# A time-mix layer and a GELU FFN in one kernel: the output projection of blocks two to seven set behind the FFN, around the next block's half chunk

## The chip, the cores and the metric

The kernel runs on one core of a Trainium2 chip. The metric is the device time of one execution in microseconds (us), the median of several runs. Engines are called as the profile calls them: PE is TensorE (matmul), PEld its weight loads, DVE is VectorE, ACT is ScalarE, POOL is GpSimd, and SP is the engine whose queue issues the DMAs.

## The reference

The input `x` is 4 x 1024 x 512, f32. It is normalised over its last axis, and two branches are computed from the result and added to `x`. The first is a time mix with a recurrence over the tokens, the second a GELU FFN with fp16 at three places.

```python
xn = layernorm(x)                                  # over 512
# branch 1, HIDDEN = 704
xx = concatenate([xn[:, 1:2], xn[:, :-1]], axis=1) - xn
k = (xn + xx * time_mix_k) @ Wk.T                  # 512 -> 704
r = (xn + xx * time_mix_r) @ Wr.T
w = exp(-exp(time_decay))
state = state * w + relu(k_t); out_t = state * r_t # a scan over the tokens
y = layernorm(out @ Wv.T) * gamma + beta           # 704 -> 512
# branch 2, N = 2048
X = xn.astype(float16)
D = gelu(X.astype(float32) @ W0.T + bias0).astype(float16)
E = (D.astype(float32) @ W1.T + bias1).astype(float16)
result = x + y + E
```

## The kernel before

The 4096 tokens are worked through in eight blocks of 512 (index `i` = 0 to 7 in the code; the text counts them from one). A block's work on PE is:

- `attention` (L361): the 704 hidden channels are five full chunks of 128 and a half chunk of 64. For each full chunk, `pk` and `pr` (L385) are products of four 128x128 pieces of the weights with 512 tokens, in f32, which the hardware runs as two matmuls each. ACT takes relu of `pk` into `rk` (L370), DVE scans it into `st` (L372), POOL copies the last state into `carry`, and DVE multiplies `st` and `pr` into `g` (L396). The half chunk puts k and r into the two halves of one bank, `both` (named `pkr`): its matmuls have 64 columns each (128*64 in the profile), one for k and one for r, on the two column halves of the array. Its result is `gh` (L408).
- `ffn` (L470): the sixteen up products `pd` (L480, f32r, eight matmuls each, weights in a high and a low part), GELU on ACT into `d16` (L488), a cast on DVE into `d` (L490), and sixteen down products onto the four banks `pe` (L495, eight matmuls each). Up runs two steps ahead of down.
- `attention_out` (L413): the projection of `g` and `gh` to 512 channels, one bank `po` for each of four stripes of 128 tokens. Full chunks are 128*128 matmuls (L420); the half chunk's have 64 rows (64*128, L430), two stripes side by side on the two row halves of the array. The order is: full chunks of stripes 0 and 1, all the half chunks, full chunks of stripes 2 and 3. `residual` then takes statistics (L183, L184), the reciprocal deviation on POOL (L177, L178) and three DVE operations (L441, L444, L445) into `z`; the first of them is the last reader of `po`.
- `finish` (L463): `pe` plus bias in fp16 (`e16`, L466), the sum with `z` (L467), and the DMA to `out`.

The dictionary `between` puts three steps into the loop over n of the FFN: at n = 0 the projection of the same block, at n = 4 the normalisation of the next block's `x` (`layernorm`, L183 to L187), at n = 7 its transposition into `xnT` (sixteen L204) and the mixed inputs `xk` and `xnT` (L348, L350). `finish` of block `i` comes behind its FFN, ahead of `attention` of block `i + 1`.

Engines run their instructions in the order given; a scheduler orders them at build time within what the tiles' dependencies allow, except in stretches of `manual_schedule`. PSUM has two pools of four banks: `ps_mm` for `pk`, `pr`, `pkr`, `pd` and `po`, and `ps_e` for `pe`. A tile takes the bank of the fourth tile before it in its pool, and its first matmul waits for that tile's last reader. `x`, `xk`, `g`, `gh` and `xnT` exist once; `xres` has two buffers, `z` four, `w1` three. The weights of down are read again from DRAM for each block (`w`, 512 KB for each n), on SP's queue, with `x`, `xres` and `out`.

Of the kernel before, what the change touches and what calls it, by code (L numbers as in the profile page):

```python
# [8 lines left out]
F16 = mybir.dt.float16  # L9
F32 = mybir.dt.float32  # L10
# [4 lines left out]
P = 128  # L15
# [4 lines left out]
def time_mix_and_gelu_ffn(  # L20
# [26 lines left out]
    nc = tc.nc  # L47
    B, T, C = x.shape
    HID = wkT.shape[1]
    N = w0T.shape[1]  # L50
    TB = 512
    NS = TB // P
    NC = C // P
# [4 lines left out]
    NF = HID // P  # L58
# [296 lines left out]
    def ffn_input(i, x16s):  # L355
        xf = wide.tile([P, NC, TB], F32R, tag="xf", name=f"xf_{i}")
        for c in range(NC):
            nc.vector.tensor_copy(xf[:, c, :], x16s[c])
        return xf

    def attention(i, xk):  # L361


        b, t0 = blocks[i]
        g = one.tile([P, NF, TB], F32, tag="g", name=f"g_{i}")
        gh = one.tile([P, NS // 2, P], F32, tag="gh", name=f"gh_{i}")

        def states(h, hw, pk):
            rk = two.tile([P, TB], F32, tag="rk", name=f"rk_{i}_{h}", bufs=1)
            nc.scalar.activation(rk[:hw], pk, AF.Relu)  # L370
            st = two.tile([P, TB], F32, tag="st", name=f"st_{i}_{h}")
            nc.vector.tensor_tensor_scan(  # L372
                st[:hw],
                w_sb[:hw, h : h + 1].to_broadcast([hw, TB]),
                rk[:hw],
                0.0 if t0 == 0 else carry[:hw, h : h + 1],
                ALU.mult,
                ALU.add,
            )
            if t0 + TB < T:  # L380
                nc.gpsimd.tensor_copy(carry[:hw, h : h + 1], st[:hw, TB - 1 : TB])
            return st

        def product(dst, w, cols, src, c):
            nc.tensor.matmul(dst, w[c][:, cols], src, start=(c == 0), stop=(c == NC - 1))  # L385

        for h in range(NF):
            cols = slice(h * P, (h + 1) * P)
            pk = ps_mm.tile([P, TB], F32, tag="mm", name=f"pk_{i}_{h}")
            for c in range(NC):  # L390
                product(pk, wk_sb, cols, xk[:, c, :], c)
            st = states(h, P, pk)
            pr = ps_mm.tile([P, TB], F32, tag="mm", name=f"pr_{i}_{h}")
            for c in range(NC):
                product(pr, wr_sb, cols, xnT[:, c, 1:], c)
            nc.vector.tensor_mul(g[:, h, :], st, pr)  # L396

        both = ps_mm.tile([P, TB], F32, tag="mm", name=f"pkr_{i}")
        for c in range(NC):
            product(both[:HF], wk_sb, slice(H0, HID), xk[:, c, :], c)  # L400
            product(both[HF:], wr_sb, slice(H0, HID), xnT[:, c, 1:], c)
        st = states(NF, HF, both[:HF])

        def tokens(ap, odd):
            return ap.rearrange("p (s two t) -> p s two t", two=2, t=P)[:, :, odd, :]

        for odd in range(2):
            nc.vector.tensor_mul(  # L408
                gh[odd * HF : (odd + 1) * HF], tokens(st[:HF], odd), tokens(both[HF:], odd)
            )  # L410
        return g, gh

    def attention_out(i, g, gh):  # L413

        b, t0 = blocks[i]
        pos = [ps_mm.tile([P, C], F32, tag="mm", name=f"po_{i}_{s}") for s in range(NS)]

        def full(s, first):
            for h in range(NF):
                nc.tensor.matmul(  # L420
                    pos[s],
                    g[:, h, s * P : (s + 1) * P],
                    wv_sb[:, h, :],
                    start=(first and h == 0),
                    stop=(not first and h == NF - 1),
                )

        def half(s, first):
            rows = slice(s % 2 * HF, (s % 2 + 1) * HF)
            nc.tensor.matmul(  # L430
                pos[s], gh[rows, s // 2, :], wv_sb[rows, NF, :], start=first, stop=not first
            )

        def residual(s):
            xr = two.tile([P, C], F32, tag="xres", name=f"xres_{i}_{s}")
            nc.sync.dma_start(xr, x[b, t0 + s * P : t0 + (s + 1) * P, :])
            mv = four.tile([P, 1, 2], F32, tag="mv1", name=f"mvy_{i}_{s}")
            stats_of(mv, 0, pos[s], f"sty_{i}_{s}")
            rstd = rstd_of(mv[:, :, 1], f"ry_{i}_{s}")
            z = four.tile([P, C], F32, tag="z", name=f"z_{i}_{s}")  # L440
            nc.vector.scalar_tensor_tensor(  # L441
                z, pos[s], mv[:, 0, 0:1], gamma_sb, ALU.subtract, ALU.mult
            )
            nc.vector.scalar_tensor_tensor(z, z, rstd, beta_sb, ALU.mult, ALU.add)  # L444
            nc.vector.tensor_add(z, z, xr)  # L445
            return z

        early, late = range(NS // 2), range(NS // 2, NS)  # L450
        for s in early:
            full(s, True)
        for s in early:
            half(s, False)
        for s in late:
            half(s, True)
        zs = [residual(s) for s in early]
        for s in late:
            full(s, False)
        zs += [residual(s) for s in late]  # L460
        return zs

    def finish(i, s, z, pe):  # L463
        b, t0 = blocks[i]
        e16 = two.tile([P, C], F16, tag="e16", name=f"e16_{i}_{s}")
        nc.vector.tensor_add(e16, pe, b1_sb)  # L466
        nc.vector.tensor_add(z, z, e16)  # L467
        nc.sync.dma_start(out[b, t0 + s * P : t0 + (s + 1) * P, :], z)

    def ffn(i, xf, between, state):  # L470


        pe = [ps_e.tile([P, C], F32, tag="pe", name=f"pe_{i}_{s}") for s in range(NS)]

        def up(n):
            pd = ps_mm.tile([P, TB], F32, tag="mm", name=f"pd_{i}_{n}")
            cols = slice(n * P, (n + 1) * P)
            for c in range(NC):
                for w in (w0h, w0l):
                    nc.tensor.matmul(  # L480
                        pd,
                        w[c][:, cols],
                        xf[:, c, :],
                        start=(c == 0 and w is w0h),
                        stop=(c == NC - 1 and w is w0l),
                    )
            d16 = two.tile([P, TB], F16, tag="d16", name=f"d16_{i}_{n}")
            nc.scalar.activation(d16, pd, AF.Gelu, bias=b0_sb[:, n : n + 1])  # L488
            d = wide.tile([P, TB], F32R, tag="d", name=f"d_{i}_{n}", bufs=4)
            nc.vector.tensor_copy(d, d16)  # L490
            return d

        def down(n, s, d, w1):
            for part in range(2):
                nc.tensor.matmul(  # L495
                    pe[s],
                    d[:, s * P : (s + 1) * P],
                    w1[part],
                    start=(n == 0 and part == 0),
                    stop=(n == NN - 1 and part == 1),  # L500
                )

        last = 3 if i == len(blocks) - 1 else 0
        AHEAD = 2
        waiting = [(up(n), load_w1(i, n)) for n in range(AHEAD)]
        for n in range(NN):
            if n in between:
                between[n]()  # L510
            if n + AHEAD < NN:
                waiting.append((up(n + AHEAD), load_w1(i, n + AHEAD)))
            if n < NN - last:
                operands = waiting.pop(0)
                for s in range(NS):
                    down(n, s, *operands)
        if last:
            with tc.manual_schedule(engines={nc.tensor.engine, nc.vector.engine}):
                for s in range(NS):
                    for n, operands in zip(range(NN - last, NN), waiting):  # L520
                        down(n, s, *operands)
                    finish(i, s, state["zs"][s], pe[s])
        return pe

    behind = ExitStack()
    x16s, xk = first_inputs(x_now, behind)
    xf = ffn_input(0, x16s)
    for i in range(len(blocks)):
        more = i + 1 < len(blocks)
        state = {}  # L530
        gs = attention(i, xk)
        if i == 0:
            for grp in range(N // W0G):
                load_w0(grp)
# [3 lines left out]
            x_now = load_x(i + 1)  # L538

        def out_stage():  # L540
            state["zs"] = attention_out(i, *gs)

        def next_norm():
            layernorm(i + 1, x_now)
# [2 lines left out]
            transposed(x_now)  # L547
            state["mixed"] = mixed_inputs(i + 1)

        between = {0: out_stage}  # L550
        if more:
            between[4] = next_norm
            between[7] = next_inputs
        pe = ffn(i, xf, between, state)
        if more:
            x16s, xk = state["mixed"]
            xf = ffn_input(i + 1, x16s)
            for s in range(NS):
                finish(i, s, state["zs"][s], pe[s])


# [41 lines left out]
```

## Time and profile before

| | us |
|---|---|
| median of 4 runs | 944.89 (944.73 to 945.22) |
| profiled execution, its own time | 944.73 |
| its span (granted PE clock 1.0 throughout) | 942.8 |
| busy: PE / PEld / DVE / ACT / POOL | 934.4 / 587.5 / 485.8 / 162.7 / 51.8 |
| `pd` (L480), two rows | 203.5 + 199.4, 1024 matmuls, mean 397 and 389 ns |
| `pe` (L495) | 251.1, 1024 matmuls, mean 389 ns |
| `pr`, `pk` (L385) | 144.2 and 144.1, 320 matmuls each, mean 592 ns |
| `po` full chunks (L420) / half chunk (L430) | 140.8, 320 matmuls / 15.9, 64 matmuls |
| `pkr` (L385), two rows | 29.2 + 29.2, 64 matmuls each, mean 598 and 599 ns |
| DMA | 106.49 MB, mean 113 GB/s |

The span is the stretch that the profile covers; the time of the execution is 1.9 us longer. Busy times of a group count overlapping matmuls of the group once, so the mean duration of a matmul (592 ns in f32) is longer than the step from one to the next; the step is read from start times. Blocks follow each other evenly: in the chain of waits `pk` of block three begins at 244.76 us, that of block four at 360.29, and so on every 115.52 us. One block's stretches, with the busy time and the instructions (x) of each engine in them:

```
core 0: us, PE busy (x) PEld busy (x) DVE busy (x) ACT busy (x) POOL busy (x), PEclk, DMA share, GB/s
244.76:279.04 34.28, 34.28 (x81) 14.81 (x79) 12.43 (x15) 2.98 (x5) 0.93 (x5) 1.00 0.18 56
279.04:282.63 3.59, 3.59 (x17) 1.07 (x16) 0.69 (x1) 0.00 (x0) 0.00 (x0) 1.00 0.02 5
282.63:286.41 3.78, 3.78 (x18) 3.11 (x17) 2.49 (x4) 1.28 (x2) 0.18 (x1) 1.00 0.01 2
286.41:305.70 19.29, 19.29 (x50) 8.20 (x49) 8.98 (x16) 0.69 (x1) 2.91 (x6) 1.00 0.11 27
305.70:360.10 54.40, 54.40 (x241) 45.06 (x240) 34.63 (x65) 11.60 (x18) 2.07 (x4) 1.00 0.50 166
```

They are: the five full chunks, the half chunk, two up products, the projection, and the rest of the FFN. PE is busy through all of them.

### The profile page before, as it was taken

Reading aid. Unit: us, or ns where it says so; the run is one execution under the profiler, and the core shown is the slowest. Engines: PE = TensorE matmul, PEld = TensorE weight load, DVE = VectorE, ACT = ScalarE, POOL = GpSimd, SP = SyncE. Lnnn points to the kernel's source line nnn. Section 1 sums busy time; section 2 is a strip of 40 time slices with the busy share of each in tenths; the row PEclk is TensorE's granted clock in tenths of the full one; section 3 lists DMA queues with packets and bytes.
Section 4 is the critical chain, followed back from the end, with each engine's and each line's share of the span. In section 5 each row is a group of like instructions: output and inputs, shape, how many; then the busy total and the mean of one; then the engine's idle time right before and its main releaser. Section 6 shows DMA issues by size and latency. Waiting matters only on the chain.

```text
span 942.8 us, 8746 instructions
## 1 busy us (share of the span) xinstructions
PE 934.4 (99%) x3260; PEld 587.5 (62%) x3260; DVE 485.8 (52%) x842; ACT 162.7 (17%) x265; POOL 51.8 (5%) x124
## 2 busy tenths in 40 slices
PE   8999999999999999999999999999999999999998
PEld 5447764488544885448854588445884458744686
DVE  6558752484425944359343592426923279332513
ACT  6323410012100220102201021010210102111021
POOL 0010000100001000011000100002000020000100
PEclk9999999999999999999999999999999999999999
DMA  9744660045401454014530155302552024510243
GB/s 296 231 138 151 226 232 0 23 134 188 147 1 24 138 197 133 1 33 159 188 111 1 38 182 167 105 0 68 185 159 81 0 89 135 161 62 1 69 154 112
DMA packets 39573, 106.49 MB, mean 113 GB/s; under 512 B 4431, under 2 KB 4460, under 8 KB 39532
## 3 DMA queue, kind: packets, MB, share of 16 engines
q1 hardware_dynamic: 39532, 105.94, 34.4%
q8 instruction: 26, 0.43, 0.2%
q14 instruction: 15, 0.12, 0.0%
HBM read 89.14 MB, written 16.78 MB: 112 GB/s over the span
## 4 chain that ended last, share of the span: by engine, by line
PE 94%; DVE 4%; issue 1%; DMA 0%; ACT 0%; POOL 0%; SPq 0%; DVEq 0%
PE pd L480 23%; PE pe L495 22%; PE po L420 15%; PE pr L385 15%; PE pk L385 15%; PE pkr L385 3%; PE po L430 2%; DVE xnT L204 1%; DVE w L125 0%; DMA x<-in_L_attn_x 0%; DVE d L490 0%; DVE z L467 0%; DVE xk L350 0%; DVE e L466 0%; DVE stx L183 0%
## 5 line engine op out<-in xcount | busy, mean ns | idle before, releaser
L495 PE MATMUL pe<-w,d 128*128 128x512 f32 x1024 | 251.1, 389 | 1.4 <-DVE w L125 0.8
L495 PEld LDWEIGHTS pe<-w,d 128*128 128x128 f32 x1024 | 192.1, 188 | 42.3 <-DVE d L490 1.5
L480 PE MATMUL pd<-xf,w0h 128*128 128x512 f32 x512 | 203.5, 397 | 0.0
L480 PE MATMUL pd<-xf,w0l 128*128 128x512 f32 x512 | 199.4, 389 | 0.0
L488 ACT ACTIVATE d<-pd,b_sb 128x512 f16<-128x512 f32 x128 | 87.9, 687 | 418.6 <-PE pd L480 408.4
L385 PE MATMUL pr<-xnT,wr 128*128 128x512 f32 x320 | 144.2, 592 | 0.0
L385 PE MATMUL pk<-xk,wk 128*128 128x512 f32 x320 | 144.1, 592 | 0.0
L420 PE MATMUL po<-wv_sb,g 128*128 128x512 f32 x320 | 140.8, 595 | 0.0
L490 DVE CAST d<-d 128x512 fp32r<-128x512 f16 x128 | 53.9, 423 | 130.2 <-ACT d L488 129.3
L480 PEld LDWEIGHTS pd<-xf,w0h 128*128 128x128 f32 x512 | 96.1, 188 | 28.0 <-issue 5.7
L480 PEld LDWEIGHTS pd<-xf,w0l 128*128 128x128 f32 x512 | 96.1, 188 | 21.4 <-issue 1.9
L385 PEld LDWEIGHTS pr<-xnT,wr 128*128 128x128 f32 x320 | 60.6, 189 | 76.9 <-issue 75.7
L420 PEld LDWEIGHTS po<-wv_sb,g 128*128 128x128 f32 x320 | 60.1, 190 | 75.7 <-issue 74.7
L385 PEld LDWEIGHTS pk<-xk,wk 128*128 128x128 f32 x320 | 60.7, 190 | 73.3 <-issue 72.0
L204 DVE STREAM_TRANSPOSE xnT<-x 32x512 f32<-32x512 f32 x112 | 78.7, 703 | 2.2
L372 DVE TENSOR_TENSOR_SCAN st<-w_sb,carry,rk 128x512 f32<-128x512 f32 (+1 forms) x24 | 30.8, 1282 | 70.3 <-ACT rk L370 70.3
L370 ACT ACTIVATE rk<-pk 128x512 f32<-128x512 f32 x40 | 23.9, 597 | 233.6 <-PE pk L385 233.6
L183 DVE BATCH_NORM_STATS2 sty<-po 128x6 f32<-128x512 f32 x32 | 22.0, 689 | 73.5 <-PE po L430 67.9
L372 DVE TENSOR_TENSOR_SCAN st<-w_sb,rk 128x512 f32<-128x512 f32 (+1 forms) x24 | 29.3, 1221 | 55.3 <-ACT rk L370 53.6
L396 DVE TENSOR_TENSOR g<-st,pr 128x512 f32<-128x512 f32 x40 | 27.4, 686 | 53.6 <-PE pr L385 53.6
L177 POOL TENSOR_SCALAR ry<-mvy 128x1 f32<-128x1 f32 x32 | 11.4, 357 | 502.3 <-DVE mvy L184 502.3
L466 DVE TENSOR_TENSOR e<-pe,b_sb 128x512 f16<-128x512 f32 x32 | 20.7, 684 | 17.0 <-PE pe L495 17.0
(75 smaller groups left out, 457.2 us busy)
## 6 DMA issues: line engine op xcount, KB each, us to landing
w<-w1d SPq DMA_DIRECT2D x111, 512.0 KB, 3.3
x<-in_L_attn_x SPq DMA_DIRECT2D x32, 256.0 KB, 3.0
xres<-in_L_attn_x SPq DMA_DIRECT2D x32, 256.0 KB, 2.6
w1d<-w SPq DMA_DIRECT2D x16, 512.0 KB, 2.9
out<-z SPq DMA_DIRECT2D x32, 256.0 KB, 5.5
w0raw<-in_L_ffn_W SPq DMA_DIRECT2D x16, 256.0 KB, 4.8
w1raw<-in_L_ffn_W SPq DMA_DIRECT2D x16, 256.0 KB, 3.6
wk<-in_L_attn_Wk SPq DMA_DIRECT2D x4, 352.0 KB, 4.4
```

What stands on the lines that cost most here:

```text
L183: nc.vector.bn_stats(st6, src)
L204: nc.vector.transpose(dst[i * Q : (i + 1) * Q, :, :, j, :], src[j * Q : (j + 1) * Q, :, :, i, :],)
L370: nc.scalar.activation(rk[:hw], pk, AF.Relu)
L372: nc.vector.tensor_tensor_scan(st[:hw], w_sb[:hw, h : h + 1].to_broadcast([hw, TB]), rk[:hw], 0.0 if t0 == 0 else carry[:hw, h : h + 1], A ...
L385: nc.tensor.matmul(dst, w[c][:, cols], src, start=(c == 0), stop=(c == NC - 1))
L396: nc.vector.tensor_mul(g[:, h, :], st, pr)
L420: nc.tensor.matmul(pos[s], g[:, h, s * P : (s + 1) * P], wv_sb[:, h, :], start=(first and h == 0), stop=(not first and h == NF - 1),)
L466: nc.vector.tensor_add(e16, pe, b1_sb)
L480: nc.tensor.matmul(pd, w[c][:, cols], xf[:, c, :], start=(c == 0 and w is w0h), stop=(c == NC - 1 and w is w0l),)
L488: nc.scalar.activation(d16, pd, AF.Gelu, bias=b0_sb[:, n : n + 1])
L490: nc.vector.tensor_copy(d, d16)
L495: nc.tensor.matmul(pe[s], d[:, s * P : (s + 1) * P], w1[part], start=(n == 0 and part == 0), stop=(n == NN - 1 and part == 1),)
```

## The change

`attention` is split into two functions, `full_chunks` and `half_chunk`, which it returns uncalled. The half chunk's bank `both` moves from `ps_mm` to `ps_e`. `attention_out` takes a function `amid` and calls it between the half chunk's matmuls and the late full chunks. `finish` is split: `rounded` makes `e16` (four buffers instead of two) and frees the bank of `pe`. For blocks two to seven `between` no longer holds the projection; behind the FFN come the four `rounded`, the next block's `xf`, the projection with the next block's half chunk in the middle, the four `finish`, and then the next block's full chunks. Block one and block eight keep their projection at n = 0 of the FFN; block two's half chunk stays behind its full chunks. The scheduler sets the steps of `between` (the next block's normalisation and transposition) anew where the engines' orders leave room: on DVE they come earlier than before, the statistics and the normalisation in the projection and the full chunks before, the transposes from the first casts of the FFN on.

```diff
@@ -361,9 +361,8 @@
     def attention(i, xk):
         b, t0 = blocks[i]
-        g = one.tile([P, NF, TB], F32, tag="g", name=f"g_{i}")
-        gh = one.tile([P, NS // 2, P], F32, tag="gh", name=f"gh_{i}")
         def states(h, hw, pk):
             rk = two.tile([P, TB], F32, tag="rk", name=f"rk_{i}_{h}", bufs=1)
@@ -384,33 +383,42 @@
         def product(dst, w, cols, src, c):
             nc.tensor.matmul(dst, w[c][:, cols], src, start=(c == 0), stop=(c == NC - 1))
-        for h in range(NF):
-            cols = slice(h * P, (h + 1) * P)
-            pk = ps_mm.tile([P, TB], F32, tag="mm", name=f"pk_{i}_{h}")
-            for c in range(NC):
-                product(pk, wk_sb, cols, xk[:, c, :], c)
-            st = states(h, P, pk)
-            pr = ps_mm.tile([P, TB], F32, tag="mm", name=f"pr_{i}_{h}")
-            for c in range(NC):
-                product(pr, wr_sb, cols, xnT[:, c, 1:], c)
-            nc.vector.tensor_mul(g[:, h, :], st, pr)
-        both = ps_mm.tile([P, TB], F32, tag="mm", name=f"pkr_{i}")
-        for c in range(NC):
-            product(both[:HF], wk_sb, slice(H0, HID), xk[:, c, :], c)
-            product(both[HF:], wr_sb, slice(H0, HID), xnT[:, c, 1:], c)
-        st = states(NF, HF, both[:HF])
+        def full_chunks():
+            g = one.tile([P, NF, TB], F32, tag="g", name=f"g_{i}")
+            for h in range(NF):
+                cols = slice(h * P, (h + 1) * P)
+                pk = ps_mm.tile([P, TB], F32, tag="mm", name=f"pk_{i}_{h}")
+                for c in range(NC):
+                    product(pk, wk_sb, cols, xk[:, c, :], c)
+                st = states(h, P, pk)
+                pr = ps_mm.tile([P, TB], F32, tag="mm", name=f"pr_{i}_{h}")
+                for c in range(NC):
+                    product(pr, wr_sb, cols, xnT[:, c, 1:], c)
+                nc.vector.tensor_mul(g[:, h, :], st, pr)
+            return g
         def tokens(ap, odd):
             return ap.rearrange("p (s two t) -> p s two t", two=2, t=P)[:, :, odd, :]
-        for odd in range(2):
-            nc.vector.tensor_mul(
-                gh[odd * HF : (odd + 1) * HF], tokens(st[:HF], odd), tokens(both[HF:], odd)
-            )
-        return g, gh
-    def attention_out(i, g, gh):
+        def half_chunk():
+            gh = one.tile([P, NS // 2, P], F32, tag="gh", name=f"gh_{i}")
+            both = ps_e.tile([P, TB], F32, tag="pe", name=f"pkr_{i}")
+            for c in range(NC):
+                product(both[:HF], wk_sb, slice(H0, HID), xk[:, c, :], c)
+                product(both[HF:], wr_sb, slice(H0, HID), xnT[:, c, 1:], c)
+            st = states(NF, HF, both[:HF])
+            for odd in range(2):
+                nc.vector.tensor_mul(
+                    gh[odd * HF : (odd + 1) * HF],
+                    tokens(st[:HF], odd),
+                    tokens(both[HF:], odd),
+                )
+            return gh
+        return full_chunks, half_chunk
+    def attention_out(i, g, gh, amid=lambda: None):
         b, t0 = blocks[i]
         pos = [ps_mm.tile([P, C], F32, tag="mm", name=f"po_{i}_{s}") for s in range(NS)]
@@ -454,16 +462,21 @@
             half(s, False)
         for s in late:
             half(s, True)
+        amid()
         zs = [residual(s) for s in early]
         for s in late:
             full(s, False)
         zs += [residual(s) for s in late]
         return zs
-    def finish(i, s, z, pe):
+    def rounded(i, s, pe):
+        e16 = four.tile([P, C], F16, tag="e16", name=f"e16_{i}_{s}")
+        nc.vector.tensor_add(e16, pe, b1_sb)
+        return e16
+    def finish(i, s, z, e16):
         b, t0 = blocks[i]
-        e16 = two.tile([P, C], F16, tag="e16", name=f"e16_{i}_{s}")
-        nc.vector.tensor_add(e16, pe, b1_sb)
         nc.vector.tensor_add(z, z, e16)
         nc.sync.dma_start(out[b, t0 + s * P : t0 + (s + 1) * P, :], z)
@@ -519,16 +532,21 @@
                 for s in range(NS):
                     for n, operands in zip(range(NN - last, NN), waiting):
                         down(n, s, *operands)
-                    finish(i, s, state["zs"][s], pe[s])
+                    finish(i, s, state["zs"][s], rounded(i, s, pe[s]))
         return pe
     behind = ExitStack()
     x16s, xk = first_inputs(x_now, behind)
     xf = ffn_input(0, x16s)
+    state = {}
+    full_chunks, half_chunk = attention(0, xk)
+    g = full_chunks()
+    gh = half_chunk()
     for i in range(len(blocks)):
         more = i + 1 < len(blocks)
-        state = {}
-        gs = attention(i, xk)
         if i == 0:
             for grp in range(N // W0G):
                 load_w0(grp)
@@ -538,7 +556,7 @@
             x_now = load_x(i + 1)
         def out_stage():
-            state["zs"] = attention_out(i, *gs)
+            state["zs"] = attention_out(i, g, gh)
         def next_norm():
             layernorm(i + 1, x_now)
@@ -547,16 +565,26 @@
             transposed(x_now)
             state["mixed"] = mixed_inputs(i + 1)
-        between = {0: out_stage}
+        within = i == 0 or not more
+        between = {0: out_stage} if within else {}
         if more:
             between[4] = next_norm
             between[7] = next_inputs
         pe = ffn(i, xf, between, state)
         if more:
             x16s, xk = state["mixed"]
+            e16s = [rounded(i, s, pe[s]) for s in range(NS)]
             xf = ffn_input(i + 1, x16s)
+            full_chunks, half_chunk = attention(i + 1, xk)
+            next_gh = []
+            if within:
+                zs = state["zs"]
+            else:
+                zs = attention_out(i, g, gh, lambda: next_gh.append(half_chunk()))
             for s in range(NS):
-                finish(i, s, state["zs"][s], pe[s])
+                finish(i, s, zs[s], e16s[s])
+            g = full_chunks()
+            gh = next_gh[0] if next_gh else half_chunk()
 # ---- launch: one core; the weights go in transposed ----
```

## The prediction

> **What bounds the kernel now.** I read the page first (busy shares, and the chain that ended last), then all waits of TensorE, then the chain again over one block, then TensorE's timeline where the tiling of the array changes. The page:
>
> ```profile
> span 942.8 us, 8746 instructions
> ...
> PE 934.4 (99%) x3260; PEld 587.5 (62%) x3260; DVE 485.8 (52%) x842; ACT 162.7 (17%) x265; POOL 51.8 (5%) x124
> ...
> PE 94%; DVE 4%; issue 1%; DMA 0%; ACT 0%; POOL 0%; SPq 0%; DVEq 0%
> ```
>
> TensorE is the bound nearly throughout. All that it waited for in the span:
>
> ```profile
> PE idle L231 <- POOL ident masks.py:199: 1.3, 1, 1.3
> PE pt L254 <- ACT x L248: 1.3, 1, 1.3
> PE pe L495 <- DVE w L125: 0.8, 1, 0.8
> PE pe L495 <- DVE d L490: 0.6, 2, 0.3
> ```
>
> (us in total, times, longest). Two lie in the prologue, two in block one's FFN and at the very end; in blocks two to seven TensorE never waits. A change there can gain only by making TensorE's own instructions take less, and can lose by creating a wait. The chain over block three's start (start, us, what) shows where its instructions take more than their step:
>
> ```profile
> 275.68 3.44 PE pr L385 x8
> 279.11 3.59 PE pkr L385 x16
> 282.70 3.87 PE pd L480 x16
> 286.58 8.59 PE po L420 x20
> 295.16 1.92 PE po L430 x8
> 297.08 8.78 PE po L420 x20
> ```
>
> An f32 product of 512 columns is two matmuls of 3.44/8 = 0.43 us. `pkr` holds 16 matmuls of half the columns which run in pairs: 8 x 0.43 = 3.44, but it took 3.59. The 16 `pd` would be 3.63 (the FFN's casts of `d` follow each other every 3.63 us, for 16 such matmuls), but took 3.87. The first 20 `po` fit (8.59); the half chunk's four pairs should be 1.72 and took 1.92; the last 20 took 8.78. The timeline shows the excess itself (start, us, instruction):
>
> ```profile
> 278.09 1.02 PE L385 MATMUL pr<-xnT,wr 128*128 128x512 f32 x2
> 279.04 0.64 PE L385 MATMUL pkr<-xk,wk 128*64 128x512 f32 x1
> ...
> 279.52 0.59 PE L385 MATMUL pkr<-xk,wk 128*64 128x512 f32 x1
> ...
> 282.10 0.59 PE L385 MATMUL pkr<-xk,wk 128*64 128x512 f32 x1
> ...
> 282.63 0.50 PE L480 MATMUL pd<-xf,w0h 128*128 128x512 f32 x1
> 282.97 0.39 PE L480 MATMUL pd<-xf,w0l 128*128 128x512 f32 x1
> 283.19 0.40 PE L480 MATMUL pd<-xf,w0h 128*128 128x512 f32 x1
> ```
>
> Into column pairs (128*64): after `pr` the next start is due at 278.09 + 2 x 0.43 = 278.95 and comes at 279.04 (+0.09); the second pair comes 0.48 after the first instead of 0.43 (+0.05): 0.14 us. Out of them: due at 282.53, comes at 282.63 (+0.10), and the second `pd` 0.34 later instead of 0.23 (+0.11): 0.21 us. Into the row pairs (64*128) 1.92 - 1.72 = 0.20, out of them 8.78 - 8.58 = 0.20. So each change of tiling costs about 0.1 us in which nothing overlaps, and then a first weight load that is not hidden: about 0.05 us where it has 64 columns, 0.1 us where it has 128. A block pays 0.14 + 0.21 + 0.20 + 0.20 = 0.75 us for four changes.
>
> **The change, part by part.** (1) *The merged excursion.* For blocks two to seven the projection (`po`) runs after the FFN, and the next block's `pkr` runs between its row pairs and the late full chunks. TensorE's order becomes: FFN, 20 `po`, row pairs, column pairs, 20 `po`, the ten full chunks. Count and kinds of matmuls are the same, and this order has three changes per merged pair where there were four: into rows (0.20), rows to columns, columns to full (its first load has 128 columns, so as out of the row pairs: 0.20). The trace of before has no change from rows straight to columns. From below it is 0 (no drain and a hidden load), from above the two dearest rows after each other, 0.20 + 0.20 = 0.40. I take 0.14, the row of another tiling into columns: the first load has the same 64 columns. New sum 0.54, saved 0.21 us, six times: **1.3 us**. With the bounds it is six times 0.35 = 2.1 us saved, or six times 0.05 = 0.3 us lost. Switches between f32 and f32r without a change of tiling cost nothing that adds up: `po` follows `pd` at 286.58 with no gap, and the first `pd` behind the late `po` ends in step.
>
> The Trainium skill, TensorEngine Tiling (Array Packing), Key Properties, says that changing the tiling mode, and not just the tile, drains the engine; by that the step from rows to columns drains too and 0 is out. TensorE: Matmul & The Clock Gate, LDWEIGHTS (loading the stationary operand), gives a load as its columns over 1.2 ns, an estimate of 53 ns for 64 and 107 ns for 128; the trace agrees (0.05 and 0.11). By the two pages the new step is about 0.15 us and the sum stays.
>
> (2) *Banks of PSUM.* `pkr` moves to the pool of `pe`. It takes the bank of `pe` 0, which the first `rounded` frees: that needs 0.68 us (L466 row) after the last down product of stripe 0, while `pkr` starts 8.59 + 1.92 = 10.5 us after the FFN. Free. The four `po` take the FFN's banks, freed by GELUs before the last downs. Then `pk` 0, `pr` 0, `pk` 1, `pr` 1 need the banks of `po` 0 to 3, which VectorE frees with L441. With 0 at the first `po`: `po` 0 is ready at about 9.8 (8.6, 0.1, and the 1.16 us that the first statistics follow the first row pair by in the trace); VectorE is idle until then, and L441 ends 2.2 and 3.7 us later as in the trace: 12.0 and 13.5. It goes on to about 16.1 with two residuals and sums, `st` and `gh` of the half chunk to 18.2 (1.23 + 0.86), and frees `po` 2 at 20.4 and, with `po` 3 ready at 23.1, that one at 25.4. TensorE asks for them at 22.9, 26.3, 29.7 and 33.2. The tightest spare is 7.8 us, so the projection's VectorE work is hidden by the late `po` and by `pk`, `pr`.
>
> (3) *VectorE behind it.* The next block's statistics and the normalisation now come between `z` 3, `st` 0 and `st` 1. They end at about 34.4 (1.48 us wait for GpSimd's power, 2.0 us for four L187), `st` 1 at 35.7; the bank that `g` 0 frees is asked for at 40. Then, once `pr` 4 has been read, four transposes stand ahead of the first cast `d` 0, which down 0 waits for:
>
> ```profile
> L204 DVE STREAM_TRANSPOSE xnT<-x 32x512 f32<-32x512 f32 x112 | 78.7, 703 | 2.2
> L490 DVE CAST d<-d 128x512 fp32r<-128x512 f16 x128 | 53.9, 423 | 130.2 <-ACT d L488 129.3
> ```
>
> From the end of `pr` 4: 0.2 until VectorE, `g` 4 0.7, four transposes 2.85, cast 0.43: 4.2 us. Down 0 comes after three up products of 1.82 us: 5.45. Spare 1.25 us, the smallest of all. Later casts have over 3 us. In block two, whose `pkr` stands last, two transposes, `st` and `gh` stand there instead: about the same 4.2.
>
> (4) *Block one's FFN* also gets the third block's statistics and normalisation on VectorE, ahead of `d` 11 and `d` 12: about 4.6 us with the wait for GpSimd. The wait of 0.8 + 0.3 us in this FFN lies earlier (107.9 to 109.2) and stays. `d` 12 and `w` 12 move from 114 and 117 to about 118.0 and 118.7; down 12 starts at 120. Spare 1.2 us.
>
> (5) *Queues.* On SP the four `xres` and four `out` issues now alternate, each waiting for VectorE, the last at about 30; what is queued behind is `w` 3 of the next FFN, which waits for down 0 at about 64 anyway; `w` 0 to 2 were issued ahead of them. The `x` loads come after `w` 4 and are read at the next block's start. GpSimd has the same instructions; its powers hold up L444 and L187 alone, and L441 frees the bank before L444. Prologue and tail are as before, and block eight keeps its projection inside the FFN.
>
> **Sum.** The profiled execution took 944.73 us (span 942.8 and 1.9 around it), 0.16 below the median of 944.89. 944.73 - 1.3 = 943.4; in terms of the median **943.6 us**. A difference under 0.2%, 1.9 us, is what a measurement of this kernel can't tell from no change, and 1.3 us is 0.14%.
>
> **The rivals.** *Free step from rows to columns.* If the column pairs start in step behind the row pairs, 2.1 us are saved: 942.8, faster by 0.22%. For it: both are pairs on halves of the array. Against: four of four changes of tiling in each block stall. *Dear step.* The step costs 0.40, as much as leaving one tiling for full chunks and entering the next: 0.3 us lost, 945.2. For it: no row shows this change; against: all four rows split into the same two pieces. *The transposes make down 0 late* (slower). Place: the first cast of the FFN of blocks two to seven. If VectorE comes to it more than 1.25 us later than I walk (a transpose held by a reader of `xnT`, or work left over from the projection), each block loses what is over; beyond 1.25 + 0.53 us per block the kernel is slower by over 0.2% (six times 0.53 are the 1.3 gained and 1.9 lost). Priced at eight transposes ahead of the cast instead of four: 2.85 - 1.25 = 1.6 us a block, 9.6 in all, 953. For it: in block one's FFN a cast was late behind work of this kind (the last wait line). Against: the walk has each instruction of that stretch. *The merge does not happen*: if the scheduler had set `pkr` elsewhere, nothing would move; its order of TensorE's instructions has it between the row pairs and the late chunks in six blocks, so under 1%.
>
> **Chances.** Forecast 65%, 943.6, by itself 943.0 to 944.2 (the step from 0.05 to 0.25). Free step 16%, and 2% for gains that I don't see: faster 18%. Dear step 6%: same 71% with the forecast. Transposes, or the 1.2 us spare of block one's FFN used up by more than 3.2 us: slower 11%. The range 942.5 to 945.4 holds both bounds of the unknown step and what the medians scatter by (0.2), and leaves out most of the slower case and the tail of the faster.
>
> **What would show it.** In the timeline of TensorE the first column pair starts 0.53 us after the last row pair (0.43 if free) and the second follows by 0.48; the first late `po` starts 0.53 after the last column pair and the second 0.53 later; `pk` to `pk` of two blocks is 115.3 us instead of 115.52. TensorE's waits list nothing for `pk`, `pr` or `pe` in blocks two to seven; an entry "pe <- DVE d" there with six or more times is the slower rival. I am wrong if the period of a block changes by anything but 0.05 to 0.35 us less.

## The result and the profile after

The median is **943.46 us** (942.84 to 943.86), against 944.84 of the kernel before in runs on the same chip: ratio 0.9985, with a 95% interval of 0.9981 to 0.999. The forecast was 943.6. The interval leaves out 1, so the gain is real, though it is smaller than the 0.2% below which the prediction held that nothing could be told: with 39 and 59 runs, 0.15% can.

The page of the profile after, span and busy times:

```profile
span 941.4 us, 8729 instructions
...
PE 933.0 (99%) x3260; PEld 587.9 (62%) x3260; DVE 486.2 (52%) x842; ACT 162.6 (17%) x265; POOL 52.6 (6%) x124
```

The span is 1.4 us shorter and so is TensorE's busy time, with the same 3260 matmuls. So the gain is in how long TensorE's own instructions take, not in a wait. Its waits (us in total, times, longest) are those of before; the two in the FFNs:

```profile
PE pe L508 <- DVE w L125: 0.8, 1, 0.8
PE pe L508 <- DVE d L503: 0.6, 2, 0.3
```

The chain at the start of block three, and over the projection of block three, the full chunks of block four and the first up products of its FFN (start, us, what):

```profile
248.28 3.43 PE pk L384 x8
...
340.70 8.59 PE po L428 x20
349.29 1.92 PE po L438 x8
351.21 3.59 PE pkr L384 x16
354.80 8.78 PE po L428 x20
363.58 3.43 PE pk L384 x8
...
397.93 5.48 PE pd L493 x24
```

The four pieces 8.59, 1.92, 3.59 and 8.78 are as long as before. What has shrunk is the piece behind the full chunks: sixteen `pd` took 3.87, 0.24 over their step; now 24 take 5.48, and 24 steps of 0.227 us (the 3.63 us of 16) are 5.45. A fourth change of tiling (a step between matmuls on the full array, pairs on its row halves and pairs on its column halves) stood there and is gone. The same piece of the chain, `pk` of one block to `pk` of the next, is now 363.58 - 248.28 = 115.30 us instead of 115.52. TensorE's timeline at the new step from rows to columns (start, us, instruction):

```profile
349.75 1.45 PE L438 MATMUL po<-wv_sb,gh 64*128 64x512 f32 x6
351.14 0.64 PE L384 MATMUL pkr<-xk,wk 128*64 128x512 f32 x1
...
351.62 0.59 PE L384 MATMUL pkr<-xk,wk 128*64 128x512 f32 x1
...
354.20 0.59 PE L384 MATMUL pkr<-xnT,wr 128*64 128x512 f32 x1
354.73 1.98 PE L428 MATMUL po<-wv_sb,g 128*128 128x512 f32 x4
```

The six row matmuls are the last three of four pairs, 0.43 us apart, the last one at 350.61. The first column pair starts 0.53 after it (0.10 more than a step) and the second 0.48 later (0.05 more). The first late `po` starts 0.53 after the last column pair; its group of four ends 1.98 us on instead of 0.59 + 3 x 0.43 = 1.88, so the 0.10 of its second load is there too.

Taken from all such places of the two traces, each change of tiling by its excess over the step, in ns. In brackets is the first part of it, before the first matmul of the new tiling; the rest lies between that one and the next:

| change | before | after |
|---|---|---|
| full to columns | 143 (93) | - |
| columns to full | 212 (103), into `pd` | 207 (103), into `po` |
| full to rows | 197 (93) | 197 |
| rows to full | 201 (97) | - |
| rows to columns | - | 147 (97) |
| sum of a block | 753 | 551 |

0.20 us a block, six times: 1.2 us. The period of a block has shrunk by 0.22 us; the 0.02 that is left is not a change of tiling. The medians differ by 1.4, with an interval of 0.9 to 1.8.

What VectorE does behind the projection, block three into block four (start, us, instruction, a wait in brackets), and TensorE's first down product of block four:

```profile
351.80 0.73 DVE L449 SCALAR_TENSOR_TENSOR z<-po,mvy,gamma_sb 128x512 f32<-128x512 f32 x1
...
365.04 0.73 DVE L449 SCALAR_TENSOR_TENSOR z<-po,mvy,gamma_sb 128x512 f32<-128x512 f32 x1
...
372.44 1.91 DVE L187 TENSOR_SCALAR x<-x,mvx,rx 128x512 f32<-128x512 f32 x4 [0.91 <-POOL rx L178]
398.57 2.84 DVE L204 STREAM_TRANSPOSE xnT<-x 32x512 f32<-32x512 f32 x4
401.44 0.43 DVE L503 CAST d<-d 128x512 fp32r<-128x512 f16 x1
```

```profile
403.25 1.07 PE L508 MATMUL pe<-w,d 128*128 128x512 f32 x4
```

L449 is the last reader of `po`: the first bank is free at 351.80 + 0.73 = 352.5 and the last at 365.8, while `pk` 0 asks for the one at 363.6 and `pr` 1 for the other at 373.9. The first cast ends at 401.87; TensorE starts down 0 at 403.25, at the end of its third up product, without a wait.

### The profile page after: what moved, and what is told of

It reads as the page before. It is cut to its first block, busy times and chain, and to the rows that moved or that the text cites. A ratio compares the mean times of both kernels' runs of the same rounds, so it can differ in the third digit from the quotient of the medians.

```text
span 941.4 us, 8729 instructions
## 1 busy us (share of the span) xinstructions
PE 933.0 (99%) x3260; PEld 587.9 (62%) x3260; DVE 486.2 (52%) x842; ACT 162.6 (17%) x265; POOL 52.6 (6%) x124
## 3 DMA queue, kind: packets, MB, share of 16 engines
q1 hardware_dynamic: 39532, 105.94, 34.2%
## 4 chain that ended last, share of the span: by engine, by line
PE 94%; DVE 4%; issue 1%; DMA 0%; ACT 0%; POOL 0%; SPq 0%; DVEq 0%
PE pd L493 23%; PE pe L508 22%; PE po L428 15%; PE pr L384 15%; PE pk L384 15%; PE pkr L384 3%; PE po L438 2%; DVE xnT L204 1%; DVE w L125 0%; DMA x<-in_L_attn_x 0%; DVE d L503 0%; DVE z L480 0%; DVE xk L350 0%; DVE e L475 0%; DVE xnT L350 0%
## 5 line engine op out<-in xcount | busy, mean ns | idle before, releaser
L384 PE MATMUL pkr<-xnT,wr 128*64 128x512 f32 x64 | 29.2, 598 | 0.0
```

## The experiments

The theory is that the gain is one change of tiling fewer in six blocks, each change costing a short drain (no new matmul starts for about 0.1 us beyond the step) and a first weight load of the new tiling that is not hidden behind another matmul. Rivals: the gain comes from the projection's new place behind the FFN, or from the half chunk's new bank; and, for what the change might have cost, VectorE's work ahead of the FFN's first cast.

**Projection behind the FFN, half chunk back behind the full chunks.** (`e1_behind_only`)

```diff
-                zs = attention_out(i, g, gh, lambda: next_gh.append(half_chunk()))
+                zs = attention_out(i, g, gh)
```

> The projection of blocks two to seven stays behind the FFN, but the next block's half chunk goes back behind its full chunks. Theory (each change of tiling costs a drain of 0.09 us and one weight load that is not hidden): four changes per block again, 0.14 + 0.21 + 0.20 + 0.20 = 0.75 us, so the whole gain of 1.3 us is gone: 944.8. Rival (the gain comes from where the projection stands, from VectorE's emptier FFN or from fewer switches between f32 and f32r): 943.5, as with the whole change.

Measured: 944.69 us, ratio to before 1.0 (0.9991 to 1.0008). The four changes are back, at 143, 214, 197 and 201 ns. The period of a block, from the starts of `pk`, is 115.48 us: 0.04 under that of before, although all four changes are there. So the projection's place gives at most these 0.04 us a block, which the medians can't tell from nothing, and no run shows where they come from; the gain comes with the merge of the half chunks.

**Only the bank.** (`e5_bank_only`, an edit of the kernel before)

```diff
-        both = ps_mm.tile([P, TB], F32, tag="mm", name=f"pkr_{i}")
+        both = ps_e.tile([P, TB], F32, tag="pe", name=f"pkr_{i}")
```

> The kernel before with one part of the change alone: the half chunk's bank comes from the pool of pe. Theory: no wait for a bank is in TensorE's list before, so nothing: 944.8. Rival (the free bank in the other pool is what gives the time): 943.5.

Measured: 944.49 us, ratio 0.9998 (0.9989 to 1.0007). The period of a block stays at 115.52 us. So the bank has no cost and no gain that can be read.

**Columns ahead of rows.** (`e2_cols_first`: `half_chunk` is cut in two, its matmuls are called ahead of the row pairs, its states and `gh` behind them)

```diff
...
             full(s, True)
+        amid()
         for s in early:
...
             half(s, True)
-        amid()
+        behind_rows()
         zs = [residual(s) for s in early]
```

> As the changed kernel, but the column pairs of the next block's half chunk come before the row pairs. Theory: still three changes, full to columns 0.14, columns to rows 0.09 + 0.11 = 0.20 (the first load has 128 columns), rows to full 0.20, sum 0.54: 943.5. Rival (a step between the two kinds of pairs has a price of its own by direction, up to 0.40 from columns to rows): up to 1.2 us more, 944.7.

Measured: 943.59 us, ratio 0.9988 (0.9979 to 0.9996). The chain over the same stretch:

```profile
349.31 3.59 PE pkr L384 x16
352.90 1.92 PE po L442 x8
354.81 8.78 PE po L432 x20
```

Full to columns cost 145 ns, columns to rows 208 (104 of it drain), rows to full 201: 554 a block, as in the changed kernel. The change into rows is dear (its weight loads have 128 columns), the one into columns cheap (64), whichever tiling is left. So the price goes by the tiling that is entered. That the load's width is the reason fits the numbers, but no run varied it by itself.

**A fourth change put back, the projection left merged.** (`e3_rows_split`: the column pairs between the row pairs of stripes 0 and 1 and those of stripes 2 and 3; `half_chunk` is cut as in the run before)

```diff
...
             half(s, False)
+        amid()
         for s in late:
             half(s, True)
-        amid()
+        behind_rows()
...
```

> As the changed kernel, but the column pairs stand between the row pairs of stripes 0 and 1 and those of stripes 2 and 3: one change of tiling more in each of six blocks and no other difference. Theory: 0.20 + 0.14 + 0.20 + 0.20 = 0.74 us a block, 1.2 us more than the changed kernel: 944.7. Rival (the gain comes from the place of the projection, not from the count of changes): 943.5.

Measured: 944.61 us, ratio 0.9998 (0.999 to 1.0007). The row pairs in the chain, now in two parts of 0.86 + 0.20:

```profile
349.67 1.06 PE po L442 x4
350.73 3.59 PE pkr L384 x16
354.31 1.06 PE po L442 x4
```

Changes of 198, 147, 209 and 201 ns, 755 a block, against 753 before; the period of a block is 115.50 us. With these four changes a block the kernel takes the time of before, although the projection stands behind the FFN. The kernel before and these four edits ran beside each other: with four changes a block 944.84 (before), 944.69, 944.49 and 944.61 us, with three 943.59.

**More transposes ahead of the first cast.** (`e6_transposes`: in blocks two to seven eight of the sixteen instead of four stand there, held by a hand-written order of VectorE)

```diff
-        waiting = [(up(n), load_w1(i, n)) for n in range(AHEAD)]
+        waiting = []
+        if first:
+            with tc.manual_schedule(engines={nc.vector.engine}):
+                first()
+                waiting = [(up(0), load_w1(i, 0))]
...
+        if ahead:
+            next_norm()
...
+        pe = ffn(i, xf, between, state, (lambda: transposed(x_now, range(2))) if ahead else None)
```

> As the changed kernel, but eight transposes instead of four are put ahead of the first cast in the FFN of blocks two to seven, by an order written out for VectorE. Theory (the spare of that cast is 1.38 us in the trace and nothing else covers it): four transposes more are 2.84 us, so the first down product waits 1.5 us in five blocks, and some 3 us in block two, whose st and gh stand there too: 10.3 us more, 953.8, with an entry pe <- DVE d of five or six times in TensorE's waits. Rival (the cast has cover that the walk does not count): 943.5.

Measured: 950.08 us (two runs), ratio 1.0054 (1.0036 to 1.0073), slower. VectorE's and TensorE's timelines in block four's FFN:

```profile
401.23 5.72 DVE L204 STREAM_TRANSPOSE xnT<-x 32x512 f32<-32x512 f32 x8
406.98 0.76 DVE L503 CAST d<-d 128x512 fp32r<-128x512 f16 x2
```

```profile
407.46 2.12 PE L508 MATMUL pe<-w,d 128*128 128x512 f32 x8 [0.71 <-DVE d L503]
```

The wait "pe <- DVE d" appears, as the rival had said, but smaller. TensorE's order here has three matmuls of the fourth up product ahead of down 0, which take up 0.68 us. It is due again at 406.59 and starts at 407.46, 0.87 late, and its eight matmuls take 0.14 longer than in step; the block's period is 116.32, 1.02 longer, against the 1.5 expected. Block two, which was to lose some 3 us, loses 1.5 (its period is 120.62 instead of 119.08). In all the kernel loses 6.6 us of the 10.3 expected. So the mechanism is real, and the price was too high, because the walk (the sum over the instructions of that stretch) held TensorE's order fixed.

**Block one merged too.** (`e4_block_one`)

```diff
-        within = i == 0 or not more
+        within = not more
```

> As the changed kernel, but block one's projection is also behind its FFN, around block two's half chunk. Theory: one change of tiling less, 0.21 us; and VectorE has some 14 us of projection work less in block one's FFN, where TensorE waits 1.4 us in all for a cast and a weight split that are late, so up to 1.4 us more: 942.0, at worst 943.2. Rival: the first cast there now stands behind st, gh and five transposes, 6.0 us after the half chunk where TensorE asks for it after 5.45, and the weights of the FFN are wanted earlier, so block one gains new waits that give it back: 943.5 or more.

Measured: 948.19 us, ratio 1.0037 (1.0023 to 1.0051). The expectation missed, in sign; its rival had the place, but only 0.55 us of wait there. Without the projection at n = 0, block one's FFN begins while VectorE still has its own half chunk and the next transposes to do, and the scheduler puts these ahead of the first cast. VectorE's timeline, then TensorE's, and TensorE's stretch by windows (us, busy PE, PEld, DVE, ACT, POOL; then the granted clock, the DMA share and GB/s):

```profile
57.63 2.13 DVE L204 STREAM_TRANSPOSE xnT<-x 32x512 f32<-32x512 f32 x3
59.79 0.76 DVE L503 CAST d<-d 128x512 fp32r<-128x512 f16 x2
```

```profile
60.27 3.68 PE L508 MATMUL pe<-w,d 128*128 128x512 f32 x8 [4.80 <-DVE d L503]
```

```profile
60.27:63.79 3.52, 3.52 (x8) 2.77 (x9) 3.40 (x6) 0.69 (x1) 0.00 (x0) 0.52 0.00 0
```

TensorE asks for the cast at 55.31 (the last `pd` starts at 55.08 and has a step of 0.23) and starts at 60.27: 4.96 us late. The eight matmuls behind it then take 3.52 us where eight take 1.81 elsewhere, at a granted clock of 0.52: another 1.7. The old wait at 108 us is gone in this kernel and one change of tiling is saved (-0.2). In the changed kernel that wait makes one `pe` start at 107.91 instead of 107.46 and the next at 109.17 instead of 108.14, 1.5 us together. 4.96 + 1.7 - 1.5 - 0.2 = 5.0, and the medians of this and the changed kernel differ by 4.7. The rival had counted 6.0 us from the end of the half chunk to the end of the first cast; here it is 60.23 - 49.79 = 10.4. VectorE makes `g` 4, whose `pr` was done at 46.20, only at 53.71, behind splits of the FFN's weights (L125, the last at 53.10), and the later FFNs have no such splits.

**The same with the casts first.** (`e8_casts_first`: block one merged, its transposes held behind the third cast)

```diff
+            if n == 2:
+                state["third"] = state["cast"]
...
-            transposed(x_now)
+            if i == 0:
+                with tc.issue_after(state["third"].ins):
+                    transposed(x_now)
+            else:
+                transposed(x_now)
...
-        within = i == 0 or not more
+        within = not more
```

> As e4_block_one, but the transposes in block one's FFN must come after its third cast on VectorE. Theory (the 4.8 us wait there, and the half clock behind it, come from the first cast standing behind five transposes): the first cast ends 1.5 us after TensorE asks, not 5, the clock stays at 1.0, and the old wait at n = 9 and one change of tiling are saved: 943.2, 5 us under e4_block_one. Rival (the wait comes from weights or the table load that the projection used to cover): it stays near 948.

Measured: 943.75 us, ratio 0.9986 (0.9976 to 0.9995). The first wait falls from 4.80 to 1.65 us (`st` and `gh` of the half chunk still stand ahead of the cast) and the granted clock of 56 to 64 us is 1.00. So the transposes were the cause of the rest of that wait, and of the low clock behind it, in the run before. It gives no more than the changed kernel: TensorE, due at 55.83, starts at 57.64, and these 1.8 us take the place of the old 1.5.

**Block one's next inputs later.** (`e7_later_inputs`: an edit of the changed kernel against its wait in block one)

```diff
-            between[7] = next_inputs
+            between[10 if i == 0 else 7] = next_inputs
```

> The changed kernel, and in block one's FFN the next block's mixed inputs are called at n = 10 instead of 7, so that VectorE makes the tenth cast and weight split before the last four to five mixing operations. Theory: TensorE's one wait in the middle of the kernel, 0.45 + 1.04 us at 108 us, goes; the later casts have 0.3 us or more to spare: 942.1 (1.3 us under the changed kernel), with no pe <- DVE w in TensorE's waits. Rival (VectorE is short in this FFN as a whole, so the wait moves to the cast or split of n = 12): 943 or more.

Measured: 942.08 us (941.67 to 942.44), ratio 0.9966 (0.9954 to 0.9979): the best version, 1.7 us under the changed kernel beside it (the next run), 1.5 of them in block one. In the changed kernel TensorE stands at down 9 of block one for `d` 9 (cast at 107.44) and then for a split of `w` (108.43), both behind mixed inputs on VectorE. Here that cast is at 105.94 and that split at 104.08, and of the FFNs' waits only the one at the end is left:

```profile
PE pe L508 <- DVE d L503: 0.3, 1, 0.3
```

**The changed kernel again,** beside the last three. (`a1_whole_again`)

> The changed kernel once more, beside e7_later_inputs on the same chip: 943.5.

Measured: 943.81 us, ratio 0.9989 (0.9981 to 0.9998). Its span was 942.0 us where the first profile had 941.4. The difference lies in the prologue: in the chain the first `pk` starts at 12.52 us instead of 11.97, and the blocks behind it take 115.30 in both. Two profiles of one kernel so differ by near half of what the change gives, and the medians and the start times inside one trace are the evidence here, not two spans.

## Why the prediction was right, step by step

- **What bounds it.** TensorE throughout, and in blocks two to seven without a wait: the same holds after. That left TensorE's own instructions as the only place of a gain, and the gain is there.
- **The price of a change of tiling.** About 0.1 us before the first matmul of the new tiling, and behind it 0.05 us where a load has 64 columns and 0.1 where it has 128: the runs without a merge, with the columns first and with the rows split show eleven means between 143 and 214 ns, and they fall in two groups by the tiling that is entered: into columns 143 to 147, into rows or full chunks 197 to 214. The row that the trace of before did not have, rows to columns, was taken as 0.14, from the likeness to the other row into columns, and is 0.147: the step on which the forecast hung was right by its reason. The saving of a block was 0.21 by the forecast and is 0.20 by the start times.
- **A term put at nothing.** The forecast held that switches between f32 and f32r cost nothing that adds up. With the projection behind the FFN they are fewer, and 0.02 of the 0.22 us by which a block's period shrank (0.04 in the run with the projection's place alone) is no change of tiling. So a little of the agreement of 1.3 us with the measured 1.4 is luck: the changes alone give 1.2, and this small rest, for which no run shows the cause, adds 0.1.
- **Free step and dear step.** Both are out: the step is neither in time with the pairs ahead of it nor the sum of two changes. The Trainium skill, TensorEngine Tiling (Array Packing), Key Properties, says that a change of the tiling mode drains the engine; the six places of this trace agree, with 97 ns each before the first column pair.
- **Banks.** Walked from the first `po` (340.62 in the trace after), the banks were to come free at 12.0, 13.5, 20.4 and 25.4 us; L449 frees them at 11.9, 13.4, 20.5 and 25.2. The tightest spare is 8.1 us (forecast 7.8). The normalisation (L187) was to end at 34.4 and ends at 374.35 - 340.62 = 33.7. The bank of `pkr` alone gave no difference.
- **The transposes and down 0.** The spare was forecast at 1.25 us and is 403.25 - 401.87 = 1.38. The rival had its place and mechanism right, as the run with eight transposes showed, but was over-priced: 1.6 us a block against 1.02, since TensorE's order filled part of it with other matmuls.
- **Block one's FFN.** Forecast: the old wait stays, and `d` 12 and `w` 12 come 1.2 us before they are needed. The wait is the same 0.8 + 0.3; `d` 12 is cast by 117.6 and `w` 12 split by 118.8, and down 12 starts at 119.96.
- **The median.** 1.3 us off the profiled execution, set on the median: 943.6 against 943.46. The rest of the difference, 0.1 us, is below what the medians scatter by.

What failed was not a step of the prediction but the first idea about extending it: that block one could be merged for nothing. The expectation walked VectorE's work there from the half chunk on, but took it that VectorE keeps up until then, as in the later blocks; in block one it was 7.5 us behind with `g` 4 (46.20 to 53.71), and the halved clock that followed was not priced at all.

Open: block one merged with `gh` too behind the first cast, and that together with the later inputs, were not tried.

## What to carry to other kernels

Where TensorE is busy throughout, list the changes of tiling in its order and read each one's excess from start times; put stretches of small tiling next to each other, since each change cost 0.14 us (into column pairs) or 0.20 to 0.21 (into row pairs or the full array) here. Before such a move, add up instruction by instruction the work of the engine that frees the banks and of the one that feeds the first matmul behind it, and do so for the first block separately, where the order differs. When TensorE's own order gives only tenths, look at the remaining waits: one due time in one block (1.5 us) was worth as much as the restructuring of six.

## What the runs showed of the hardware that was not expected

- After 4.8 us without a matmul, TensorE ran its next 3.5 us at a granted clock of 0.52: eight matmuls at 0.43 us each instead of 0.23. Waits of 0.7 and 1.65 us in other runs left it at 1.00. So this stall cost its own length and about 1.7 us more. The Trainium skill, TensorE: Matmul & The Clock Gate, Part 1, gives an idle window of about 3.4 us behind which the clock is halved; these waits lie on both sides of it, and agree.
- A wait on TensorE also costs a little behind it (the 0.14 above): the eight matmuls after the 0.71 us wait took 409.42 - 407.46 = 1.96 us from their first start to that of the next product, where eight in step take 1.82. The length of the wait hardly matters: behind 1.65 us (the casts first) and behind 0.34 us (the end of the changed kernel) it is 1.95. Some 0.11 us of it lie between the first and the second start, as much as behind a change of tiling into 128 columns, though the tiling stays: this fits a weight load that is hidden in a running stream and not at the start of one.
